# Moving one tile's industry product, stacking two-part operands on rows, and reordering the last tile of a layer in a four-layer graph kernel

## The chip, the cores and the metric

The kernel runs on one core of a Trainium2 chip. The metric is the device time of one execution in microseconds. A core has five engines that run side by side, each through its own instructions in order: TensorE (PE, with its weight loads shown apart as PEld), VectorE (DVE), ScalarE (ACT), GpSimd (POOL) and SyncE (SP), which here issues the DMA transfers. An engine waits at an instruction until the semaphores that it names are reached, and whatever stands behind that instruction on the same engine waits too.

## The reference, cut to what matters

There are B = 8 samples of N = 2048 nodes with C = 64 channels, and one sparse adjacency of 2048 x 2048, normalised by rows. Four layers follow each other, each as `x = layernorm(x + layer(x))`.

```python
# layer 0: Chebyshev terms T0=I, T1=A, T2=2AA-I, weights made per node from an embedding
w = einsum('nd,dkio->nkio', embedding, weight); x_g = einsum('knm,bmc->bnkc', A_stack, x)
out = einsum('bnki,nkio->bno', x_g, w) + bias
# layer 1: attention over 64 hyperedges (H: 2048 x 64), then "industry" against "g"
h = x @ W;  s = leaky_relu(h @ a_node)
alpha = softmax(where(H.T, s, NEG)); agg = einsum('ben,bnf->bef', alpha, h)   # per hyperedge
beta = sigmoid((h @ a_gn)[node] + (agg @ a_ge)[edge])
all_he = elu(beta * h + (1 - beta) * agg)                                     # per edge and node
he = elu(agg); se = tanh(he @ fcW + fcb) @ av; coefs1 = softmax(where(H, se, NEG))
g = einsum('bne,benf->bnf', coefs1, all_he)
industry = einsum('nm,bmf->bnf', adj / deg, x @ W_ind)
pair = stack([industry, g]); out = softmax(tanh(pair @ fcW + fcb) @ av) weighted sum of pair
# layer 2: x @ Ws + (adj @ x) @ Wn + b;   layer 3: (Dinv (adj + I) Dinv @ x) @ W.T
```

## The kernel before, in words

**Tiles.** A tile is 128 nodes (P), so there are NT = 16 of them; a tile's row of 8 samples times 64 channels is BC = 512 columns. Each large product takes its one operand as a 0/1 mask of the adjacency (a tile of it, 128 columns against all nodes, is 1 MB in a DRAM scratch, loaded by `mask_tile`, L1337) and the other as a pair "hi" and "lo" whose sum is the float32 value: each part is exact in TensorE's single-pass float32 format (`r_`, F32R), so two passes give full precision. A tile's industry product is therefore 32 matmuls of 128x128 by 128x512 (16 row blocks times two parts, `times_mask`).

**Stages in order.**

1. `first_product` and `memberships` (L306 on). The masks and layer 0's first product are made. Meanwhile, by quarters of 512 nodes, lists are built and stored in DRAM scratch: for each node its first to fourth hyperedge as one-hot columns (`oh01`: first and second, 64 rows each; `oh23`: third and fourth), a one-hot `S` for memberships beyond, and the transposed membership `pT`.
2. `layer0` (L923). A loop over j = 0..16 with steps g = 0..7 works on tile j (weights and sums, `weigh`) and finishes tile j-1 (`normed`, `to_features`, `scores`) and tile j-2 (`project`, `gather`). `scores` gives es, the exponentials of s; `project` (L1144) gives `h` and the pair y_hi, y_lo of x @ W_ind; `gather` (L1182) adds a tile to `aggp`, the numerator of agg; `denominators` (L1197) adds the 16 tiles' es to `denp`. In the last round, j = 16, denp's first 15 tiles stand at g = 1, behind `spread`, which makes the membership operands.
3. Stage 1 of `layer1` (L535 to L600): one chain over the 64 hyperedges, with each step on another engine. agg (DVE), he (ACT exponential, DVE), `trhe` (PE), heT (ACT), `fche` (PE), the (ACT tanh), `sep` (PE, 16 matmuls of one column), ese (DVE, ACT), its pair ese2 (DVE), `dnp` (PE, 16 matmuls), rec (ACT, DVE) and `hgr` (DVE reciprocal, L598). Beside it, `halves` splits agg + 1 and -agg into pairs, and `ext` collects two columns per sample for each hyperedge.
4. The turns of `layer1`. A string of steps (`turns`, L878) is run for t = 0..18; in turn t, tile t+1's unit (hyperedges to g), tile t's industry product, and the mixing and norm of tiles t-1 to t-3 go side by side. Tile 0's unit and the head of tile 1's go ahead of turn 0. A unit begins with `sx` (L633 to L637: the one-hots against ext, S against hgr) and goes on with `gp` in two halves (L680: a one-hot of 64 rows against the pair of agg, for two of the four lists side by side on rows 0 to 63 and 64 to 127), three DVE operations `d` each, `dp` (L705: float32 part; L707: the fourth list against the pair of -agg), exponentials, and sums on POOL. The industry's result is read by DVE's `dlt` (L750), which frees its accumulator for the next tile.
5. The tail of layer 1 makes layer 2's operands tile by tile (`tr`, `u`, L850, and the pair y_hi, y_lo, L858 and L860). Layers 2 and 3 (L1340 on) are 16 tiles each of 32 mask matmuls, and a norm.

**What sets the order.** `program_order` (L196) pins the order of PE, DVE, ACT and POOL to the order in which the program is written, inside layer 0's loop, stage 1 and the turns. SyncE's order is left to the scheduler. A transfer into on-chip memory waits until everything that used that memory is finished; pools opened one after another share memory, and buffers of one tag alternate in it. The PSUM accumulators are allotted in the same way.

A branch on `flag` chooses this program where no node has too many memberships; `bad` and `badp` (L1393) are part of that check.

Of the kernel before, what the change touches and what calls it, by code (L numbers as in the profile page):

```python
# [18 lines left out]
P = 128  # L19
# [32 lines left out]
def kernel(  # L52
# [176 lines left out]
    def lists_flag(box, tot, pm, w, an, avc):  # L229
# [56 lines left out]
        for k, shape in (  # L286
            ("oh01", [P, QW]), ("oh23", [P, QW]), ("S", [P, 4, P]), ("pT", [E, QW])
        )
# [6 lines left out]
    def memberships(pre, ps, pm, fcw_sb, fcb_sb, fcg_sb):  # L295
# [26 lines left out]
        raws = {}  # L322

# [22 lines left out]
        for q in range(NQ):  # L346

            raw = raws.pop(q)
            pT = pre.tile([P, QW], F32, tag="pT", name=f"pT_{q}")
            nc.vector.tensor_scalar(r_(pT), raw, 0.0, None, op0=ALU.is_gt)  # L350
            nc.sync.dma_start(lists["pT"][q], pT[0:E])
            yield
            pf = ps.tile([P, QW], F32, tag="li", name=f"pf_{q}")
            nc.tensor.matmul(
                pf, r_(tri.rearrange("p h e -> p (h e)")), r_(pT[0:E]), start=True, stop=True
            )
            yield
            pfm = raw
            nc.vector.tensor_tensor(pfm, pf, pT, ALU.mult)
            oh01 = pre.tile([P, QW], F32, tag="oh01", name=f"oh01_{q}")  # L360
            nc.vector.tensor_scalar(r_(oh01), pfm, order01, None, op0=ALU.is_equal)
            nc.sync.dma_start(lists["oh01"][q], oh01)
            oh23 = pre.tile([P, QW], F32, tag="oh23", name=f"oh23_{q}")
            nc.vector.tensor_scalar(r_(oh23[0:64]), pfm[0:64], 3.0, None, op0=ALU.is_equal)
            if q + 1 < NQ:
                load(q + 1)
            S = pre.tile([P, 4, P], F32, tag="S", name=f"S_{q}")
            yield
            for t in range(4):

                j = 4 * q + t
                cols = slice(t * P, (t + 1) * P)
                sm = ps.tile([P, QW], F32, tag="li", name=f"sm_{j}")
                nc.tensor.matmul(
                    sm[:, 0:E], r_(pT[0:E, cols]), r_(tri[:, 0, :]), start=True, stop=True
                )
                nc.vector.tensor_scalar(
                    r_(S[:, t, :]), iota[:, 0, :], base3[:, j:j + 1], None, op0=ALU.is_ge
                )
                nc.vector.scalar_tensor_tensor(  # L380
                    r_(S[:, t, :]), iota[:, 0, :], end3[:, j:j + 1], S[:, t, :],
                    op0=ALU.is_lt, op1=ALU.mult,
                )
                yield
                rk = pre.tile([P, 2, E], F32, tag="rk", name=f"rk_{j}")
                for h in range(2):
                    nc.vector.scalar_tensor_tensor(
                        r_(rk[:, h, :]), sm[:, 0:E], base3[:, j:j + 1], pm[:, j, :],
                        op0=ALU.add, op1=ALU.mult,
                    )  # L390
                yield
                nc.tensor.matmul(
                    sm[:, P:2 * P], r_(rk.rearrange("p h e -> p (h e)")), r_(S[:, t, :]),
                    start=True, stop=True,
                )
                yield
                nc.vector.tensor_tensor(
                    r_(oh23[64:128, cols]), sm[64:128, P:2 * P], iota[64:128, 1, :], ALU.is_equal
                )
            nc.sync.dma_start(lists["oh23"][q], oh23)  # L400
            nc.sync.dma_start(lists["S"][q], S)
            yield
# [92 lines left out]
    def layer1(  # L495
        stack, own, wts, fcw_sb, fcb_sb, av_sb, fcg_sb, vecs, rden, hgr, aggp, agg_st, h_sb,
        i_hi, i_lo, mask_tile, times_mask, w2_sb, bias2_sb,
# [8 lines left out]

        oh01 = l1.tile([P, N], F32, tag="oh01", name="oh01")
        oh23 = l1.tile([P, N], F32, tag="oh23", name="oh23")

        S = l1.tile([P, NT, P], F32, tag="S", name="S")  # L510

        agg_hi, agg_lo = (
# [6 lines left out]
        ext = l1.tile([P, 2, 2, B], F32, tag="ext", name="ext")  # L519

        with tc.tile_pool(name="fa", bufs=2) as fa:
            pT = fa.tile([E, N], F32, tag="pT", name="pT", bufs=1)
            for q in range(NQ):
                cols = slice(q * QW, (q + 1) * QW)
                nc.sync.dma_start(pT[:, cols], lists["pT"][q])
                nc.sync.dma_start(oh01[:, cols], lists["oh01"][q])
                nc.sync.dma_start(S[:, 4 * q:4 * q + 4, :], lists["S"][q])
                nc.sync.dma_start(oh23[:, cols], lists["oh23"][q])
# [5 lines left out]
            with program_order():  # L534
# [5 lines left out]
                nagg_hi, nagg_lo = (  # L540
                    own.tile([P, BC], F32, tag=f"b0_{k}", name=f"nagg_{k}") for k in (11, 15)
                )

                def halves(hi, lo, f, c):
                    s = slice(0 if c else 64, P)
                    nc.vector.tensor_scalar(r_(hi[s]), agg[s], f, c, op0=ALU.mult, op1=ALU.add)
                    full = fa.tile([P, BC], F32, tag="full", name="full", bufs=1)
                    nc.vector.tensor_scalar(full[s], agg[s], f, c, op0=ALU.mult, op1=ALU.add)
                    nc.vector.tensor_tensor(r_(lo[s]), full[s], hi[s], ALU.subtract)

                nc.vector.tensor_scalar(he, he, 1.0, -1.0, op0=ALU.min, op1=ALU.add)
                nc.vector.tensor_tensor(he, he, agg, ALU.max)
                tr = ps_tr.tile([P, NP, P], F32, tag="tr", name="trhe")
# [4 lines left out]
                halves(agg_hi, agg_lo, 1.0, 1.0)  # L558
# [10 lines left out]
                nc.gpsimd.memset(ext, 0.0)  # L569
# [9 lines left out]
                halves(nagg_hi, nagg_lo, -1.0, 0.0)  # L579
                ese2 = fa.tile([P, 2, B], F32, tag="ese2", name="ese2", bufs=1)  # L580
                nc.vector.tensor_copy(r_(ese2[:, 0, :]), ese)
                nc.vector.tensor_tensor(r_(ese2[:, 1, :]), ese, ese2[:, 0, :], ALU.subtract)

                dn = ps_tr.tile([P, NT, 2, B], F32, tag="tr", name="dnp")
# [5 lines left out]
                for h in range(2):  # L590
                    s = slice(h * 64, (h + 1) * 64)
                    nc.vector.tensor_reduce(ext[s, h, 0, :], b_view(he)[s], AX.X, ALU.add)
                    nc.vector.tensor_copy(ext[s, h, 1, :], ese[s])
# [29 lines left out]
        ps_acc = stack.enter_context(tc.tile_pool(name="fi", bufs=1, space=PSUM))  # L623
        ps_fc = stack.enter_context(tc.tile_pool(name="ff", bufs=1, space=PSUM))
        extv = ext.rearrange("p u k b -> p (u k b)")

        def units(j, dst):

            cols = slice(j * P, (j + 1) * P)
            sm = ps_s.tile([P, QW], F32, tag="sm", name=f"sx_{j}")  # L630

            for i in range(2):
                nc.tensor.matmul(  # L633
                    sm[:, P + 32 * i:P + 32 * i + 32], (oh01, oh23)[i][:, cols], extv,
# [40 lines left out]
            for i in range(2):  # L675
                gp = ps_g.tile([P, 2, BC], F32, tag="g", name=f"gp_{j}_{i}")
                for u in range(2):
                    rs = slice(u * 64, (u + 1) * 64)
                    for part in (agg_hi, agg_lo):
                        nc.tensor.matmul(  # L680
                            gp[:, u, :], r_((oh01, oh23)[i][rs, cols]), r_(part[rs]),
                            start=part is agg_hi, stop=part is agg_lo,
                        )
# [18 lines left out]
                if i == 0:  # L702
# [3 lines left out]
                    for part in (nagg_hi, nagg_lo):  # L706
                        nc.tensor.matmul(  # L707
                            dp, r_(oh23[64:128, cols]), r_(part[64:128]),
                            start=False, stop=part is nagg_lo,
                        )  # L710
# [25 lines left out]
        def industry(j):  # L736

            a = mask_tile(mjp, j, "l1")
            acc = ps_acc.tile([P, BC], F32, tag="acc", name=f"ind_{j}")
            for mt in range(NT):  # L740
                times_mask(acc, a, i_hi, i_lo, mt)
# [181 lines left out]
    def layer0(  # L923
# [6 lines left out]
        h_sb, wb, wa, vecs, av_sb, pm, es, hgr, aggp, rden = layer1s  # L930
# [157 lines left out]
        def normed(j, step):  # L1088
# [10 lines left out]
            elif step == 1:  # L1099
                var = tile("var", f"var_l0_{j}", (P, B))  # L1100
                nc.vector.tensor_reduce(var, b_view(norm[j]), AX.X, ALU.add)
                std = tile("std", f"std_l0_{j}", (P, B))
                nc.scalar.activation(std, var, AF.Sqrt, bias=eps_t)
                norm[j] = std
            else:
                rstd = tile("rstd", f"rstd_l0_{j}", (P, B))
                nc.vector.reciprocal(rstd, norm[j])
# [36 lines left out]
        def project(j):  # L1144
# [23 lines left out]
            nc.scalar.copy(r_(by_half(hi)), mm[:, :, :, C:2 * C])  # L1168
            nc.scalar.copy(by_half(h_sb[:, j, :]), mm[:, :, :, 0:C])
# [30 lines left out]

        denp = []
# [17 lines left out]
        with program_order():  # L1219
# [6 lines left out]
            for j in range(NT + 1):  # L1226
# [4 lines left out]
                for g in range(8):  # L1231
                    when(j, weigh, g)
                    if g == 0:
                        when(j - 1, normed, 0)
# [4 lines left out]
                    elif g == 1:  # L1239
                        when(j - 1, normed, 1)  # L1240
                        if j == NT:
                            denp.append(ps_acc.tile([P, BC], F32, tag="acc", name="denp")[:, 0:B])
                            spread()
                            denominators(0, NT - 1)
                        if first:
# [23 lines left out]
                    elif g == 6:  # L1269
# [4 lines left out]
                        else:  # L1274
                            denominators(NT - 1, NT)
# [5 lines left out]
            project(NT - 1)  # L1281
# [3 lines left out]
    def short_program(top):  # L1285
# [69 lines left out]
        agg_st = ExitStack()  # L1355
        with tc.tile_pool(name="l0", bufs=1) as l0, tc.tile_pool(
# [10 lines left out]
            h_sb = buffer(own, 1, "h")  # L1367
            aggp = agg_st.enter_context(tc.tile_pool(name="fag", bufs=1, space=PSUM)).tile(
                [P, BC], F32, tag="agg", name="aggp"
            )  # L1370
            with tc.tile_pool(name="l0s", bufs=2) as l0s, tc.tile_pool(
                name="accs0", bufs=1, space=PSUM
            ) as ps_acc, tc.tile_pool(name="trs0", bufs=2, space=PSUM) as ps_tr, tc.tile_pool(
# [4 lines left out]
                    y_hi, y_lo, (h_sb, wb, wa, vecs, av_sb, pm, es, hgr, aggp, rden),  # L1378
# [22 lines left out]
            y_lo, mask_tile, times_mask, w2_sb, bias2_sb,  # L1401
        )

# [671 lines left out]
```

## Time and profile before

| | us |
|---|---|
| three runs | 1355.73, 1354.02, 1349.54 |
| their median | 1354.02 |
| the profiled execution's own time | 1355.84 |
| its span in the trace | 1354.0 |
| PE busy in the span | 1287.4 (95%) |
| DVE busy | 917.9 (68%) |
| ACT busy | 367.0 (27%) |
| POOL busy | 443.7 (33%) |

The profiled execution has a span (first to last instruction) and a time of its own that is 1.8 us longer. Stages on the span's scale: layer 0 until about 699, its last tile until 720, stage 1 until 739, the turns until about 1047, the tail of layer 1 until 1086, layers 2 and 3 until the end. Each engine's busy time is given as a share of the span; the clock of TensorE as it was granted is a row of its own, in tenths of full speed; over the whole span it is 0.962. A name such as `gp<-agg,oh` reads "writes gp from agg and oh"; L680 is a line of the program. In a group, `x4` is four instructions; "idle before" names who released the engine.

### The profile page before, as it was taken

The page shows a single profiled execution, that of the slowest core. Times are in us where ns is not written, and L with a number is a line of the kernel's source. Part 1 is how long each engine was busy: PE and PEld are TensorE (multiplying, and loading weights), DVE is VectorE, ACT ScalarE, POOL GpSimd, SP SyncE. Part 2 cuts the span into 40 slices and gives each one's busy share as a digit, 9 for nine tenths or more (in the row PEclk, how much of TensorE's full clock was granted, in tenths as well). Part 3 has the DMA queues.
Part 4 walks back from the last instruction along what each step waited for, and adds up shares of the span by engine and source line. Part 5 has one row for each costly group of instructions (what it writes and reads, how often), then busy time and mean ns, then how long its engine had stood idle before and what let it go on. Part 6 is the DMA issues. An engine that isn't in the chain of part 4 may idle for free.

```text
span 1354.0 us, 19969 instructions
## 1 busy us (share of the span) xinstructions
PE 1287.4 (95%) x7788; PEld 1006.0 (74%) x7788; DVE 917.9 (68%) x1591; ACT 367.0 (27%) x840; POOL 443.7 (33%) x372
## 2 busy tenths in 40 slices
PE   6999999999999999999986799999998899999996
PEld 4777788888888888888874466666666678888885
DVE  3555378787877777777663677888884656655454
ACT  2100102112112222222221346666655611111111
POOL 2000354444444444444210455555663510000000
PEclk8999999999999999999985699999998899999999
DMA  9866432333333333331604121112220223334452
GB/s 217 264 193 193 150 112 89 104 104 104 104 105 104 104 104 104 104 104 55 233 25 155 55 78 68 66 62 78 78 79 1 94 93 125 124 119 140 169 186 73
DMA packets 91221, 153.02 MB, mean 113 GB/s; under 512 B 12272, under 2 KB 55664, under 8 KB 84848
## 3 DMA queue, kind: packets, MB, share of 16 engines
q1 hardware_dynamic: 88640, 147.45, 33.4%
q10 hardware_dynamic: 2304, 4.20, 0.8%
q8 instruction: 64, 1.05, 0.3%
q14 instruction: 37, 0.30, 0.1%
q0 software_dynamic: 176, 0.02, 0.1%
HBM read 115.98 MB, written 35.66 MB: 112 GB/s over the span
## 4 chain that ended last, share of the span: by engine, by line
PE 88%; DVE 5%; DMA 3%; ACT 2%; issue 1%; POOL 0%; SPq 0%; ACTq 0%; DVEq 0%; POOLq 0%
PE pp L1073 24%; PE a L1345 17%; PE ind L1345 10%; PE y2p L1036 9%; PE y1p L471 6%; PE fc L785 3%; PE df L794 2%; DMA xraw<-in_xn 2%; PE gp L680 2%; PE aggp L1182 1%; PE try L154 1%; PE trm L154 1%; PE yp L1433 1%; PE sgp L1130 1%; PE red L730 1%
## 5 line engine op out<-in xcount | busy, mean ns | idle before, releaser
L1084 DVE SCALAR_TENSOR_TENSOR r<-pp,emb_sb,r 128x256 f32<-128x256 f32 x512 | 247.3, 483 | 115.0 <-PE pp L1073 101.3
L1073 PE MATMUL pp<-w_sb,xT 64*128 64x256 f32 x1024 | 160.6, 390 | 1.7 <-DVE r L1084 1.7
L1073 PE MATMUL pp<-w_sb,y1T 64*128 64x256 f32 x1024 | 153.7, 376 | 0.0
L1073 PE MATMUL pp<-w_sb,y2T 64*128 64x256 f32 x1024 | 153.7, 376 | 0.0
L1022 POOL TENSOR_TENSOR r<-xs,bn 128x256 f32<-128x256 f32 x32 | 22.7, 731 | 385.7 <-issue 245.0
L471 PE MATMUL y1p<-x_hi,m 128*128 128x512 f32 x256 | 106.3, 415 | 14.1 <-ACT x_hi L418 13.3
L1073 PEld LDWEIGHTS pp<-w_sb,xT 64*128 64x128 f32 x1024 | 94.6, 187 | 25.0 <-issue 14.9
L721 POOL TENSOR_TENSOR ez<-ez,coef 128x1024 f32<-128x1024 f32 x32 | 65.0, 2032 | 139.2 <-DVE ez L719 116.8
L1073 PEld LDWEIGHTS pp<-w_sb,y1T 64*128 64x128 f32 x1024 | 99.9, 187 | 10.7
L1073 PEld LDWEIGHTS pp<-w_sb,y2T 64*128 64x128 f32 x1024 | 99.8, 187 | 10.8
L1345 PE MATMUL ind<-y_hi,mj_l 128*128 128x512 f32 x256 | 106.6, 416 | 0.4 <-DVE dlt L750 0.3
L1036 PE MATMUL y2p<-y_hi,msk 128*128 128x512 f32 x256 | 103.0, 402 | 0.0
L471 PE MATMUL y1p<-x_lo,m 128*128 128x512 f32 x256 | 103.0, 402 | 0.0
L1345 PE MATMUL a<-y_hi,mj_l 128*128 128x512 f32 x256 | 101.3, 396 | 0.6 <-ACT y_hi L858 0.6
L1345 PE MATMUL a<-y_lo,mj_l 128*128 128x512 f32 x256 | 101.3, 396 | 0.0
L1036 PE MATMUL y2p<-y_lo,msk 128*128 128x512 f32 x256 | 101.3, 396 | 0.0
L1345 PE MATMUL ind<-y_lo,mj_l 128*128 128x512 f32 x256 | 101.2, 395 | 0.0
L1345 PE MATMUL a<-v_hi,mj_l 128*128 128x512 f32 x256 | 100.2, 392 | 0.0
L1345 PE MATMUL a<-v_lo,mj_l 128*128 128x512 f32 x256 | 100.1, 392 | 0.0
L978 POOL TENSOR_TENSOR ms<-msk,srow 128x1024 f32<-128x1024 f32 x32 | 89.9, 2809 | 4.4 <-DVE ms L991 4.4
L1345 PEld LDWEIGHTS ind<-y_hi,mj_l 128*128 128x128 f32 x256 | 48.6, 190 | 32.8 <-issue 18.8
L471 PEld LDWEIGHTS y1p<-x_hi,m 128*128 128x128 f32 x256 | 49.5, 194 | 26.9 <-ACT x_hi L418 13.8
(265 smaller groups left out, 2393.7 us busy)
## 6 DMA issues: line engine op xcount, KB each, us to landing
mj_l<-mask SPq DMA_DIRECT2D x48, 1024.0 KB, 4.9
raw<-in_at SPq DMA_DIRECT2D x32, 512.0 KB, 4.7
adj<-in_at SPq DMA_DIRECT2D x64, 256.0 KB, 3.8
mask<-msk SPq DMA_DIRECT2D x32, 512.0 KB, 4.4
xraw<-in_xn SPq DMA_DIRECT2D x8, 512.0 KB, 5.3
oh<-oh SPq DMA_DIRECT2D x16, 256.0 KB, 3.7
xT<-in_xt SPq DMA_DIRECT2D x16, 256.0 KB, 3.0
xs<-in_xn SPq DMA_DIRECT2D x16, 256.0 KB, 2.9
```

Of the source, the lines that this page charges most:

```text
L154: nc.tensor.matmul(dst, src, ident, start=True, stop=True, is_transpose=True)
L471: nc.tensor.matmul(accs[q][jj], r_(m[:, t, jj * P:(jj + 1) * P]), r_(part[:, mt, :]), start=i + h + t == 0 and part is x_hi, stop=i == 3 a ...
L680: nc.tensor.matmul(gp[:, u, :], r_((oh01, oh23)[i][rs, cols]), r_(part[rs]), start=part is agg_hi, stop=part is agg_lo,)
L721: nc.gpsimd.tensor_tensor(by_b(ez), by_b(ez), per_b(coef, 2 * i, 2), ALU.mult)
L785: nc.tensor.matmul(fc[:, h, :], fcw_sb[rs], sT[rs], start=True, stop=True)
L794: nc.tensor.matmul(df[:, b:b + 1], th[:, b % 2, (b // 2) * P:(b // 2 + 1) * P], av_sb, start=True, stop=True,)
L978: nc.gpsimd.tensor_tensor(ms, m, srow[j].unsqueeze(1).to_broadcast([P, 8, P]), ALU.mult)
L1022: nc.gpsimd.tensor_tensor(r[:, 4 * bq * C:4 * (bq + 1) * C] .rearrange("p (h l c) -> p h l c", h=2, l=2), swapped(terms[j]["xs"], bq), bn. ...
L1036: nc.tensor.matmul(acc, r_(msk[j, mt // 8][:, mt % 8, :]), r_(part[:, mt, :]), start=mt == 0 and part is y_hi, stop=mt == NT - 1 and part ...
L1073: nc.tensor.matmul(pp[:, h, pl, :], terms[j][name][rs, 2 * bq + pl], w_sb[rs, k, dq * 4 * C:(dq + 1) * 4 * C], start=k == 0, stop=k == K - 1,)
L1084: nc.vector.scalar_tensor_tensor(rb, ppv[:, :, dd, :], emb_sb[:, j, d:d + 1], rb, op0=ALU.mult, op1=ALU.add)
L1345: nc.tensor.matmul(acc, r_(a[:, mt, :]), r_(part[:, mt, :]), start=mt == 0 and part is hi, stop=mt == NT - 1 and part is lo,)
```

## The change: what it does

1. **Lists.** `oh01` and `oh23` of a quarter become one list `oh` of 128 rows by 4 tiles by 4 one-hots by 128 nodes. Each one-hot of 64 rows is stored twice, in rows 0 to 63 and in rows 64 to 127, by `store`. The eight loads of the whole lists before stage 1 go; each unit loads its own tile, 256 KB, into one of four buffers of the pool `fw`.
2. **Stacked parts.** agg + 1, -agg and ext are kept as one tile each, with the rounded value in rows 0 to 63 and the residual in rows 64 to 127. A `gp` half becomes two matmuls of 128 rows for four of 64, `dp`'s second part one for two, and `sx`'s products with ext four in the single-pass format for two in float32.
3. **Industry's tile 0.** Its 32 matmuls leave turn 0. Its mask is loaded in four pieces into buffers of layer 0, and `go_on(n)` issues n pairs: 5 behind denp's first part, 3 ahead of the last gather, 4 ahead of trhe, 1 ahead of fche, 2 ahead of sep, 1 ahead of dnp. Its accumulator's pool lives from layer 0 through the turns, and denp takes a slot of layer 0's projection pool.
4. **Layer 0's last tile.** `spread` stands one step earlier (g = 0); project(15) stands right behind scores(15), and copies `h` ahead of y_hi; the norm's 1/sqrt is DVE's addition of EPS and GpSimd's power, where the other tiles use ScalarE's root and DVE's reciprocal.
5. **Small ones.** The split of -agg stands behind dnp's issue; ext is formed in a tile `sums` and split by `parts`; GpSimd's memset of ext goes.

```diff
+        def store(q, oh, first):
+            for h in range(2):
+                for u in range(2):
+                    nc.sync.dma_start(
+                        lists["oh"][q][h * 64:(h + 1) * 64, :, first + u, :],
+                        oh[u * 64:(u + 1) * 64].rearrange("e (t n) -> e t n", t=4),
+                    )
...
-            nc.sync.dma_start(lists["oh01"][q], oh01)
+            store(q, oh01, 0)
...
-            nc.sync.dma_start(lists["oh23"][q], oh23)
+            store(q, oh23, 2)
...
-                def halves(hi, lo, f, c):
-                    s = slice(0 if c else 64, P)
-                    nc.vector.tensor_scalar(r_(hi[s]), agg[s], f, c, op0=ALU.mult, op1=ALU.add)
+                def parts(dst, full):
+                    nc.vector.tensor_copy(r_(dst), full)
+                    nc.vector.tensor_tensor(r_(dst[low]), full[low], dst[low], ALU.subtract)
+                def scaled_parts(dst, f, c):
                     full = fa.tile([P, BC], F32, tag="full", name="full", bufs=1)
-                    nc.vector.tensor_scalar(full[s], agg[s], f, c, op0=ALU.mult, op1=ALU.add)
-                    nc.vector.tensor_tensor(r_(lo[s]), full[s], hi[s], ALU.subtract)
+                    nc.vector.tensor_scalar(full, agg, f, c, op0=ALU.mult, op1=ALU.add)
+                    parts(dst, full)
...
+                early[0](4)
                 tr = ps_tr.tile([P, NP, P], F32, tag="tr", name="trhe")
...
-                halves(agg_hi, agg_lo, 1.0, 1.0)
+                scaled_parts(agg1, 1.0, 1.0)
+                early[0](1)
                 fc = ps_mm.tile([P, 2, QW], F32, tag="mm", name="fche")
...
-                nc.gpsimd.memset(ext, 0.0)
+                early[0](2)
                 sp = ps_tr.tile([P, QW], F32, tag="sm", name="sep")
...
-                halves(nagg_hi, nagg_lo, -1.0, 0.0)
                 ese2 = fa.tile([P, 2, B], F32, tag="ese2", name="ese2", bufs=1)
...
+                sums = fa.tile([P, 2, B], F32, tag="sums", name="sums", bufs=1)
+                nc.vector.tensor_reduce(sums[:, 0, :], b_view(he), AX.X, ALU.add)
+                nc.vector.tensor_copy(sums[:, 1, :], ese)
+                parts(ext, sums)
+                early[0](NT)
                 dn = ps_tr.tile([P, NT, 2, B], F32, tag="tr", name="dnp")
...
+                scaled_parts(nagg, -1.0, 0.0)
...
         def units(j, dst):
-            cols = slice(j * P, (j + 1) * P)
+            oh = small("oh", f"oh_{j}", (P, 4, P), 4)
+            nc.sync.dma_start(oh, lists["oh"][j // 4][:, j % 4])
...
-            for i in range(2):
+            for u in range(4):
                 nc.tensor.matmul(
-                    sm[:, P + 32 * i:P + 32 * i + 32], (oh01, oh23)[i][:, cols], extv,
+                    sm[:, P + 16 * u:P + 16 * u + 16], r_(oh[:, u, :]), r_(extv),
...
-                    rs = slice(u * 64, (u + 1) * 64)
-                    for part in (agg_hi, agg_lo):
-                        nc.tensor.matmul(
-                            gp[:, u, :], r_((oh01, oh23)[i][rs, cols]), r_(part[rs]),
-                            start=part is agg_hi, stop=part is agg_lo,
-                        )
+                    nc.tensor.matmul(
+                        gp[:, u, :], r_(oh[:, 2 * i + u, :]), r_(agg1), start=True, stop=True
+                    )
...
-                    for part in (nagg_hi, nagg_lo):
-                        nc.tensor.matmul(
-                            dp, r_(oh23[64:128, cols]), r_(part[64:128]),
-                            start=False, stop=part is nagg_lo,
-                        )
+                    nc.tensor.matmul(dp, r_(oh[:, 3, :]), r_(nagg), start=False, stop=True)
...
         def industry(j):
-            a = mask_tile(mjp, j, "l1")
-            acc = ps_acc.tile([P, BC], F32, tag="acc", name=f"ind_{j}")
+            if j:
+                a = mask_tile(mjp, j, "l1")
+                acc = ps_acc.tile([P, BC], F32, tag="acc", name=f"ind_{j}")
+            else:
+                acc = early[1]
             for mt in range(NT):
-                times_mask(acc, a, i_hi, i_lo, mt)
+                if j:
+                    times_mask(acc, a, i_hi, i_lo, mt)
...
+                if j == NT - 1:
+                    nc.vector.tensor_scalar(var, var, EPS, None, op0=ALU.add)
+                    rstd = tile("rstd", f"rstd_l0_{j}", (P, B))
+                    nc.gpsimd.tensor_tensor(rstd, var, mhalf, ALU.pow)
+                    norm[j] = rstd
+                    return
...
+            for q, home in enumerate((4, 6, 13, 14)):
+                m = own.tile([P, 4, P], F32, tag=f"b0_{home}", name=f"m0_{q}")
+                nc.sync.dma_start(m, masks[0][:, 4 * q:4 * q + 4, :])
...
                         if j == NT:
-                            denp.append(ps_acc.tile([P, BC], F32, tag="acc", name="denp")[:, 0:B])
-                            spread()
+                            denp.append(
+                                ps_p.tile([P, 2, 2, 4 * C], F32, tag="pp", name="denp")[:, 0, 0, 0:B]
+                            )
                             denominators(0, NT - 1)
+                            early.extend(industry_early())
+                            early.pop(0)(5)
...
                         else:
+                            project(NT - 1, h_first=True)
                             denominators(NT - 1, NT)
                             gather(NT - 2)
...
-            project(NT - 1)
+            early[0](3)
             gather(NT - 1)
```

## Prediction

> **What bounds the kernel now.** I read the slices of the span first, then the chain of waits from 699 to 772 us, the windows of equal length around it, TensorE's timeline in one steady turn, and SyncE's issues. Times are microseconds of the span.
>
> ```profile
> PE   6999999999999999999986799999998899999996
> PEclk8999999999999999999985699999998899999999
> PE 88%; DVE 5%; DMA 3%; ACT 2%; issue 1%; POOL 0%; SPq 0%; ACTq 0%; DVEq 0%; POOLq 0%
> ```
>
> The second line is the granted TensorE clock in tenths. PE is nearly always busy; the one hole is at slices 21 to 23 (710 to 765 us), where busy share and clock both fall. That is the chain from the end of layer 0 to the first turns of layer 1, and most of the change lands there.
>
> ```profile
> 702.76 0.63 ACT sq_l L1097
> ...
> 709.76 1.28 ACT L1142
> ...
> 713.86 3.13 issue
> 717.02 1.05 POOL hs L1177
> 718.12 2.09 PE aggp L1182 x2
> 720.21 2.71 issue
> ...
> 738.36 0.96 DVE hgr L598
> 739.37 0.61 PE sx L637 x2
> ...
> 755.62 1.23 PE gp L680 x4
> ...
> 761.39 3.71 PE ind L1345 x8
> ```
>
> Columns: start, duration, what. L1142 is a table load; the 3.13 us of "issue" is project(15) behind the gather of tile 14. Eight industry matmuls cost 3.71 us, 0.46 each; where the clock is full they start 0.228 apart.
>
> ```profile
> 700.36:703.77 3.41, 3.29 (x36) 3.08 (x35) 2.53 (x5) 0.99 (x2) 0.00 (x0) 1.00 0.19 68
> 703.77:707.18 3.41, 1.11 (x4) 0.67 (x4) 1.96 (x5) 2.40 (x5) 1.04 (x1) 0.50 0.10 35
> ...
> 761.80:765.21 3.41, 3.41 (x10) 2.18 (x11) 1.23 (x1) 2.60 (x11) 1.35 (x1) 0.50 0.00 0
> 765.21:768.62 3.41, 3.41 (x15) 2.22 (x16) 2.60 (x3) 0.00 (x0) 1.84 (x2) 1.00 0.00 0
> ```
>
> Columns: window, length, busy time of PE, PEld, DVE, ACT, POOL, clock, DMA share, GB/s. The clock changes on a grid of 3.41 us. It halved at 703.77 after a window that PE filled for 3.29 us, but mostly with `denp`'s matmuls of 8 columns (699.04 to 702.49); it came back at 765.21 after a window filled with 512-column industry matmuls. So what counts is columns streamed: I work with "falls after a window under about half filled by wide matmuls, returns after one filled throughout".
>
> ```profile
> 843.94 0.73 PE L680 MATMUL gp<-agg,oh 64*128 64x512 f32 x4
> ...
> 848.44 0.73 PE L707 MATMUL dp<-nagg,oh 64*128 64x512 f32 x2
> 849.18 0.50 PE L1345 MATMUL ind<-y_hi,mj_l 128*128 128x512 f32 x1
> ```
>
> A steady turn takes 17.42 us (gp at 843.94, next at 861.36) and PE is full. But the industry group at 849.18 also needs DVE's dlt, which ended at 849.12 (848.38 + 0.74): both routes from gp to the industry tie within 0.06 us.
>
> **The change, part by part** (sum against the profiled run, 1355.84 us for a span of 1354.0; it stands 1.8 above the median 1354.02).
>
> *A, layer 0's tail until aggp's end (720.19).* Ten industry matmuls stand after denp, hp_15 right behind the scores, six between the two gathers; POOL's power (row L823: 1.67) and an addition replace table load 1.28 + root 0.30 + reciprocal 0.20; the table load before es goes. At full clock: denp ends 702.49, ten industry 2.3, hp_14 1.16; x1 is ready at var's end 704.1 + 0.17 + 1.67 + two halves 0.8 = 706.7; trx 0.58, xT 0.6, sgp 0.95, hp_15 1.16, denp 0.3, aggp 1.03, six industry 1.4, aggp 1.03: about 713.75, so -6.4. At half clock from 703.77: the ten industry end at 705.6, hp_14 2.08, trx 1.11, xT 0.7, sgp 1.87, hp_15 2.08, denp 0.60, aggp 2.0, industry 2.56, aggp 2.07: 720.7, so +0.5. denp fills its window with narrow matmuls as before, so I take the fall and **0** (-6.4 to +1.8, the upper end if all ten run slow).
>
> *B, aggp's end to hgr (19.1 us before).* The dense stretch denp to aggp (714 to 720.7) brings the clock back about where stage 1 begins. Then trhe gains 0.55, fche 1.04, sep 1.8, and ese2 no longer stands behind nagg's three operations on DVE (731.90 to 733.38): 1.5. agg starts 0.8 later, because DVE gets the badp and flag operations ahead of it, whose PE part now follows aggp. dnp follows sep's narrow matmuls, so I leave it slow. Sum **-4.1**; all slow it is 0 (the -1.5 eaten by 0.8 and by industry groups of 0.86 to 1.7 that outlast the waits of 0.73 and 1.27 they fill), all at full clock -6.
>
> *C, oh_0's load.* The list was resident; now each unit loads 256 KB. The compiled order of waits shows that oh_0's issue waits for hgr, the last operation of stage 1, since the buffer takes memory that stage 1 holds.
>
> ```profile
> 739.44 0.79 SPq L1340 DMA_DIRECT2D mj_l<-mask  x2
> ...
> 1070.43 1.27 SPq L1340 DMA_DIRECT2D mj_l<-mask  x3
> ```
>
> SyncE's timeline above, the page's row of DMA issues below (KB each, median us to landing):
>
> ```profile
> oh<-oh SPq DMA_DIRECT2D x16, 256.0 KB, 3.7
> ```
>
> Before, the mask issue had that wait (739.44, just behind hgr's 739.31) and nobody needed it until 761. sx_0 needs oh_0 at once: issue 0.1, landing 3.0 to 3.7 (rows of 256 KB), then sx on ext (1.06 at half clock), which before lay ahead of hgr. **+4.3** (3.0 to 4.9). Later units load a turn or more ahead and cost nothing.
>
> *D, turns 0 and 1.* Without industry, turn 0 (16.77 us) is its unit's own chain: about -1.4, since gp of the next unit stood 0.8 behind its DVE release and gp1 of this one stood behind the eight slow industry matmuls. But those matmuls brought the clock back. Now turn 1 starts slow: its rows from 772.32 to 777.81, 5.5 us, take 9.2, and part of eight industry matmuls 0.20 more each: +5. **+3.6** (-1.4 if the clock is up anyway, to +5.5).
>
> *E, fourteen further turns.* gp: four matmuls occupy 0.67, two full ones 0.34 + 0.23 = 0.57 by the industry's rows (one switch, one follow-up). dp's second part: 0.74 to about 0.3. sx on ext: 0.36 to 0.44 (four narrow ones at 0.11, as df). PE's route to the industry shrinks by 0.47, but DVE's (gp, three d of 1.23, dlt) only by gp's 0.1, and it ties; gp1 gives another 0.1 behind it. Per turn 0.2 to 0.3: **-3.6** (-1.5, up to -14 if all 0.95 counted). Three turns (809, 898, 987) took 19.0 because the clock dropped for one window; a turn near 17.15, almost five windows, drifts less against that grid: **-3** (-4.7 to +5).
>
> The Trainium skill, "TensorEngine Tiling (Array Packing)", Tiling Modes, speaks against the stacking: tiles of 64 rows execute in parallel, so two half-height pairs cost what two full matmuls do. The row of 0.67 for four (not 4 x 0.228) agrees; by the page alone gp would gain nothing, by the row 0.1.
>
> *F, the first mask of layer 2.* By the order of waits its issue now waits for u_15, the last matmul of layer 1 (ends 1085.27), in place of POOL's rstd_15; it went out at 1070.43, and layer 2 started at 1085.88. A megabyte takes 4.9 (median of 48), the least I found 4.8: +4.3, with nothing else for PE. A gap of 4.9 always leaves a window under half filled; the clock falls and the next filled window ends 3.7 to 7.1 us after the restart, which costs half of it: 1.85 to 3.55. **+7.0** (4.3 to 8.2).
>
> The Trainium skill, "TensorE: Matmul & The Clock Gate", Part 1, has half rate after an idle window of 3413 ns on a free-running grid. The grid agrees; the window up to 703.77 was not idle, and there the measurement decides. By the page this gap holds a whole idle window in (4.9 - 3.41)/3.41, 4 of 10 phases, and F would be about 5.4.
>
> *G, the lists' stores.* 24 more issues at 0.33 us on SP at 60 to 110 us, with runs of 512 B; the raw loads run two ahead: **+1** (0 to 3).
>
> Sum: 0 - 4.1 + 4.3 + 3.6 - 3.6 - 3 + 7 + 1 = +5.2, so 1361.0.
>
> **Rivals.**
> 1. *The turns are bound by PE alone* (other side: no longer slower). Then each turn gives 0.95, -13.3 in place of -3.6: 1351. For it: PE is 256 of 258 us busy from 772 to 1030, DVE 206. Against: the tie at 849.12, and turn 1's industry waited 0.26 for dlt. It decides from 0.65 per turn.
> 2. *The fill keeps the clock up* through A and B: -12.4 in place of -4.1: 1352.7. For it: 26 dense matmuls in the gaps. Against: denp's 3.45 us of narrow matmuls ahead of them, sep's behind. Both together: 1343.
> 3. *The fill does not do what it says*: matmuls at 0.43 delay trx and trhe, A +1.8, B 0, G +3: 1369.
>
> **How the numbers follow.** Forecast 0.50 (own range 1354 to 1367), rival 1 0.14, rival 2 0.16, both 0.05, rival 3 0.15. 0.5%, about 6.8 us, is what a measurement of this kernel can tell: faster is below 1347.2, slower above 1360.8. Faster: both rivals, a third of each alone, a little of the forecast's tail: 0.19. Slower: somewhat over half of the forecast, rival 3: 0.43. Same: 0.38. Range 1346 to 1369: low takes in rivals 1 and 2, high rival 3.
>
> **What would show it.** After: hgr about 735, then a SyncE issue behind it and gp_0 over 4 us later (C); the clock at half until turn 1's industry (D); SyncE's first layer-2 mask issued at u_15's end, PE idle near 5 us, and eight or more slow matmuls behind it (F); steady turns of 17.1 to 17.2 with DVE's dlt as releaser of the industry (E); fewer than three half-clock windows in 772 to 1030. Wrong if gp_0 starts before 737, if layer 2 starts within 1 us of u_15, or if turns fall below 16.8.

## The result, and the profile after

The changed kernel took 1351.13 us (median of 12 runs, 1346.22 to 1358.69), the kernel before 1354.08 (12 runs, 1349.54 to 1359.3). The ratio is 0.9984, with a 95% interval of 0.9967 to 1.0002: no difference that this measurement can tell, where 1361 was forecast. The profiled execution after took 1354.48, its span is 1352.5.

The page of the kernel after, the same three rows (busy share of PE, granted clock, chain):

```profile
PE   6999899999999999999997599999998799999997
PEclk8999899999999999999986599999998899999999
PE 85%; DVE 8%; DMA 3%; ACT 2%; issue 1%; SPq 0%; POOL 0%; ACTq 0%; DVEq 0%; POOLq 0%
```

The hole around slice 22 is there as before, and DVE's share of the whole chain has grown from 5% to 8%. The chain of waits through the hole (start, duration, what):

```profile
700.06 4.15 PE denp L1212 x30
704.21 4.47 PE ind L1229 x10
...
728.08 1.95 PE sep L576 x16
...
731.08 3.52 PE dnp L594 x16
...
735.50 0.96 DVE hgr L603
...
737.90 3.73 DMA oh<-oh
...
771.41 1.19 PE gp L685 x2
...
774.84 2.01 PE fc L789 x4
...
778.95 1.86 PE ind L1395 x8
```

The ten early industry matmuls ran at half clock (4.47 us, 0.45 each), sep ran at full clock (1.95; 3.58 before), dnp at half, and behind hgr stands a DMA that was not in the chain before. In turn 1, from 771.41, fc is slow and the industry is fast: 1.86 for eight.

Set side by side on each span's own scale, with the shift that had built up by each landmark (the letters are the terms of the forecast):

| landmark | before | after | shift | step |
|---|---|---|---|---|
| denp starts | 699.04 | 699.99 | +0.95 | |
| aggp ends | 720.19 | 720.69 | +0.50 | A -0.45 |
| hgr ends | 739.31 | 736.45 | -2.86 | B -3.4 |
| gp of unit 0 | 740.20 | 741.11 | +0.91 | C +3.8 |
| gp, turn 0 | 755.62 | 755.38 | -0.24 | unit 0 -1.15 |
| gp, turn 1 | 772.32 | 771.41 | -0.91 | turn 0 -0.7 |
| gp, turn 2 | 790.02 | 790.43 | +0.41 | turn 1 +1.3 |
| gp, turn 14 | 1003.93 | 996.32 | -7.61 | twelve turns -8.0 |
| last u of layer 1 ends | 1085.25 | 1077.23 | -8.02 | |
| layer 2 starts | 1085.87 | 1082.24 | -3.63 | mask +4.4 |
| end | 1354.02 | 1352.48 | -1.54 | restart +2.1 |

So a gain of 8 us in the later turns and 3.9 in the chain is for the most part given back at two places, where a transfer is waited for. SyncE's and PE's timelines of the second one:

```profile
1077.38 15.56 SPq L1390 DMA_DIRECT2D mj_l<-mask  x4
```

```profile
1076.07 1.16 PE L854 MATMUL u<-w_sb,xT 64*128 64x128 f32 x16 [0.42 <-DVE y_lo L864]
1082.24 0.76 PE L1395 MATMUL a<-y_hi,mj_l 128*128 128x512 f32 x1 [5.01 <-DMA mj_l<-mask]
1082.80 0.63 PE L1395 MATMUL a<-y_lo,mj_l 128*128 128x512 f32 x1
...
1088.33 0.40 PE L1395 MATMUL a<-y_hi,mj_l 128*128 128x512 f32 x1
```

The last u ends at 1077.23, the mask is issued at 1077.38, and the first matmul that needs it starts 4.86 later; then fourteen matmuls run at half clock until 1088.3.

### The profile page after: what moved, and what is told of

Its sections match the earlier page's. It is cut to its first block, busy times and chain, and to the rows that moved or that the text cites. A ratio compares the mean times of both kernels' runs of the same rounds, so it can differ in the third digit from the quotient of the medians.

```text
span 1352.5 us, 19863 instructions
## 1 busy us (share of the span) xinstructions
PE 1273.8 (94%) x7708; PEld 1009.9 (75%) x7708; DVE 917.2 (68%) x1592; ACT 363.9 (27%) x837; POOL 445.2 (33%) x372
## 4 chain that ended last, share of the span: by engine, by line
PE 85%; DVE 8%; DMA 3%; ACT 2%; issue 1%; SPq 0%; POOL 0%; ACTq 0%; DVEq 0%; POOLq 0%
PE pp L1077 24%; PE a L1395 18%; PE y2p L1040 9%; PE ind L1395 9%; PE y1p L478 8%; PE df L798 2%; PE fc L789 2%; DMA xraw<-in_xn 2%; DVE d L698 1%; DVE d L702 1%; DVE d L694 1%; PE gp L685 1%; PE try L154 1%; PE yp L1485 1%; PE hp L1165 1%
## 5 line engine op out<-in xcount | busy, mean ns | idle before, releaser
L1077 PEld LDWEIGHTS pp<-w_sb,xT 64*128 64x128 f32 x1024 | 94.4, 186 | 25.1 <-issue 14.9
L1395 PE MATMUL ind<-y_hi,mj_l 128*128 128x512 f32 x240 | 97.5, 406 | 6.9 <-DVE dlt L754 6.9
L1395 PE MATMUL ind<-y_lo,mj_l 128*128 128x512 f32 x240 | 94.5, 394 | 0.0
L1395 PEld LDWEIGHTS ind<-y_hi,mj_l 128*128 128x128 f32 x240 | 45.4, 189 | 35.5 <-DVE dlt L754 14.4
```

The lines of the kernel that those rows point to most:

```text
L1077: nc.tensor.matmul(pp[:, h, pl, :], terms[j][name][rs, 2 * bq + pl], w_sb[rs, k, dq * 4 * C:(dq + 1) * 4 * C], start=k == 0, stop=k == K - 1,)
L1395: nc.tensor.matmul(acc, r_(a[:, mt, :]), r_(part[:, mt, :]), start=mt == 0 and part is hi, stop=mt == NT - 1 and part is lo,)
```

## The experiments

All ratios are against the kernel before on the same chip, five rounds each. Between two variants I compare ratios, with 0.001 = 1.35 us; each has an interval of some +-0.002 to 0.003.

**e1: unit 0's one-hots in a buffer of their own.**

```diff
+        oh0 = l1.tile([P, 4, P], F32, tag="oh0", name="oh0")
...
+            nc.sync.dma_start(oh0, lists["oh"][0][:, 0])
...
-            oh = small("oh", f"oh_{j}", (P, 4, P), 4)
-            nc.sync.dma_start(oh, lists["oh"][j // 4][:, j % 4])
+            if j:
+                oh = small("oh", f"oh_{j}", (P, 4, P), 4)
+                nc.sync.dma_start(oh, lists["oh"][j // 4][:, j % 4])
+            else:
+                oh = oh0
```

> The changed kernel, with the first unit's one-hots loaded into a buffer of their own ahead of stage 1, so that nothing waits for hgr. Theory (the load is a wait of its own): gp_0 starts 1.0 us behind hgr's end in place of 4.65 (741.11 - 736.46), the clock is still at half there, and the time falls by about 3.7 against the changed kernel. Rival (the wait covers another): sx waits for ext, S or ScalarE in its place and gp_0 moves by under 1 us; or gp_0 moves by 3.7 but turn 1 starts slower, and under 1 us of it reaches the first turn at full clock.

Measured: 1343.52, ratio 0.9925 (0.9898 to 0.9953), 8 us under the changed kernel. PE's timeline:

```profile
731.08 1.02 PE L645 MATMUL sx<-ext,oh 128*128 128x16 f32 x4
733.23 0.60 PE L649 MATMUL sx<-hgr,S 128*128 128x16 f32 x2 [1.13 <-DVE hgr L605]
...
733.78 1.20 PE L690 MATMUL gp<-agg,oh 128*128 128x512 f32 x2
```

sx on ext is ahead of hgr again, and gp starts 0.61 behind hgr's end (733.17) in place of 4.66: -4.05, so the load was a wait of its own. Stage 1 was shorter as well, 13.62 in place of 15.76. DVE's timelines, after and then e1, tell 0.8 of that:

```profile
720.84 0.16 DVE L1445 TENSOR_SCALAR bad<-badp 128x1 f32<-128x1 f32 x1 [3.82 <-PE badp L1444]
...
721.50 0.69 DVE L537 TENSOR_TENSOR agg<-aggp,rden 128x512 f32<-128x512 f32 x1
```

```profile
719.59 0.69 DVE L539 TENSOR_TENSOR agg<-aggp,rden 128x512 f32<-128x512 f32 x1 [2.45 <-PE aggp L1202]
720.20 0.15 DVE L1450 TENSOR_SCALAR bad<-badp 128x1 f32<-128x1 f32 x1
```

The flag's operations, whose place the scheduler chooses, stand behind agg here and ahead of it after. Another 1.25 is dnp, which ran mostly at full clock (2.18 in place of 3.58; DVE's split of -agg, until 731.61, then ends last in its place). One profile can't tell if that is more than the place of the clock's windows. The profiled run took 1348.41, 4.9 above the median of the eight, and its span is 6.1 under that of the profile after. So of the 8 us by the runs the trace shows 4.05 for the load and 2.1 for stage 1; what the rest is, it can't show.

**e2: the first mask of layer 2.**

```diff
-        with tc.tile_pool(name="mj2", bufs=3) as mjp, tc.tile_pool(
+        with tc.tile_pool(name="mj2a", bufs=1) as mja, tc.tile_pool(
+            name="mj2b", bufs=1
+        ) as mjb, tc.tile_pool(name="mj2c", bufs=1) as mjc, tc.tile_pool(
...
-                a = mask_tile(mjp, j, "l2")
+                a = mask_tile((mja, mjb, mjc)[j % 3], j, "l2")
...
-                a = mask_tile(mjp, j, "l3")
+                a = mask_tile((mja, mjb, mjc)[(NT + j) % 3], j, "l3")
```

> The changed kernel, with three single-buffer pools for the masks of layers 2 and 3, so that the first one overlaps only memory that is free once the last unit is done. Theory: the first mask is issued 14 us or more ahead of u_15's end, layer 2 starts within 1 us of u_15 at full clock, idle time of 4.4 and some 2 us of slow matmuls behind it go: -6.5 against the changed kernel. Rival (only the idle goes, the clock falls there anyway, since it had been at half until 1071): -4.4. Second rival: the earlier transfer collides with the tail's, which then ends later, and nothing is gained.

Measured: 1344.6, ratio 0.992 (0.9889 to 0.9951), 8.7 under the changed kernel. SyncE, then PE:

```profile
1061.70 14.41 SPq L1390 DMA_DIRECT2D mj_l<-mask  x3
```

```profile
1074.10 1.16 PE L854 MATMUL u<-w_sb,xT 64*128 64x128 f32 x16 [0.42 <-DVE y_lo L864]
1075.88 0.47 PE L1395 MATMUL a<-y_hi,mj_l 128*128 128x512 f32 x1 [0.63 <-ACT y_hi L862]
```

The wait is gone, and the first matmul runs at full clock. From the last u's end to the end of the span it is 268.4 us, against 275.25 after: -6.8, which is the price that the forecast gave step F (7.0). The other 2.0 us between the two spans lie ahead of the last u. Both rivals fall.

**e3: both.** The edits of e1 and e2 together.

```diff
+            nc.sync.dma_start(oh0, lists["oh"][0][:, 0])
...
+                a = mask_tile((mja, mjb, mjc)[j % 3], j, "l2")
```

> Both edits, the one-hots of unit 0 and the three mask pools. Theory: they lie 340 us apart and add up, -10 against the changed kernel, 1341 or so, faster than both kernels. Rival (either is taken back by a later wait): between -4 and -7.

Measured: 1337.54, ratio 0.9874 (0.9844 to 0.9905): faster than both kernels, 14.9 under the changed one. Within the intervals the two add up (8.0 + 8.7), and neither is taken back.

**e7: gp in halves again.**

```diff
-                    nc.tensor.matmul(
-                        gp[:, u, :], r_(oh[:, 2 * i + u, :]), r_(agg1), start=True, stop=True
-                    )
+                    rs = slice(u * 64, (u + 1) * 64)
+                    for part in (agg1, agg2):
+                        nc.tensor.matmul(
+                            gp[:, u, :], r_(oh[rs, 2 * i + u, :]), r_(part[rs]),
+                            start=part is agg1, stop=part is agg2,
+                        )
```

> The changed kernel with gp alone as before (four matmuls of 64 rows for two of 128, from a pair agg1, agg2); dp and sx stay stacked. Theory (a switch between half-height and full-height matmuls costs about 0.1 on each side, and only gp1 counts, because the DVE chain ties at gp0): the steady turn goes from 16.96 back to 17.3 to 17.4. Rival (dp's second part gives the turn's gain): it stays near 17.0 to 17.1. By the forecast's own rows (0.1 for gp1): 17.05.

Measured: 1356.3, ratio 1.0026 (1.0000 to 1.0051), 5.7 over the changed kernel, with intervals that just touch; the steady turn takes 17.46, as before the change (17.42), against 16.96. The whole gain of the turn is gp's, and none is dp's or sx's. PE's timelines around gp1, in e7 and then after:

```profile
852.89 0.39 PE L1401 MATMUL ind<-y_lo,mj_l 128*128 128x512 f32 x1
853.21 0.74 PE L690 MATMUL gp<-agg,oh 64*128 64x512 f32 x4
853.87 0.50 PE L1401 MATMUL ind<-y_hi,mj_l 128*128 128x512 f32 x1
854.21 0.40 PE L1401 MATMUL ind<-y_lo,mj_l 128*128 128x512 f32 x1
```

```profile
846.59 0.50 PE L1395 MATMUL ind<-y_hi,mj_l 128*128 128x512 f32 x1 [0.57 <-DVE dlt L754]
...
848.31 0.40 PE L1395 MATMUL ind<-y_lo,mj_l 128*128 128x512 f32 x1
848.54 0.62 PE L685 MATMUL gp<-agg,oh 128*128 128x512 f32 x2
849.00 0.40 PE L1395 MATMUL ind<-y_hi,mj_l 128*128 128x512 f32 x1
849.24 0.39 PE L1395 MATMUL ind<-y_lo,mj_l 128*128 128x512 f32 x1
```

From the last industry matmul ahead of gp to the second one behind it are 1.32 us in e7 (0.32 + 0.66 + 0.34) and 0.93 after (0.23 + 0.46 + 0.24). Half-height matmuls cost about 0.1 at each change of shape, into them and out of them, beside 0.2 of their own. The first line after shows the tie that the forecast saw: the industry waits 0.57 for DVE's dlt, so dp's saving and most of gp0's are lost there.

**e4: no early industry.** industry(0) as before, in turn 0; everything else as changed.

```diff
-                            early.extend(industry_early())
-                            early.pop(0)(5)
...
-            if j:
-                a = mask_tile(mjp, j, "l1")
-                acc = ps_acc.tile([P, BC], F32, tag="acc", name=f"ind_{j}")
-            else:
-                acc = early[1]
+            a = mask_tile(mjp, j, "l1")
+            acc = ps_acc.tile([P, BC], F32, tag="acc", name=f"ind_{j}")
```

> The changed kernel with industry's tile 0 back in turn 0, as one mask of 1 MB; stacking and the tail's order stay. Theory (the fill removes PE work from turn 0, whose unit is bound by its own chain, and keeps the clock up only in parts of stage 1): aggp ends 2 to 3 us earlier than in the changed kernel, hgr 0 to 2 us later, turn 0 takes 16.5 to 17 in place of 16.0, turn 1 about 17.3 in place of 19.0; the sum is within 2 us of the changed kernel. Rival (the fill is what brings stage 1's clock back, worth 4 or more): aggp to hgr takes 18 to 19 in place of 15.8 and the time rises by 3 or more.

Measured: 1349.03, ratio 0.9961 (0.9936 to 0.9987). aggp ends 19.85 behind denp's start (20.70 after), stage 1 takes 17.84 (15.76), turns 0 and 1 take 15.22 and 17.35 (16.03 and 19.02). In the windows (length, busy PE, PEld, DVE, ACT, POOL, clock, DMA share, GB/s) of turns 0 and 1, with the turn in which the clock came back in two parts, e4 first, then after:

```profile
755.05:760.80 5.75, 5.75 (x16) 4.18 (x17) 5.48 (x6) 0.48 (x3) 3.15 (x2) 0.51 0.00 0
760.80:770.27 9.47, 8.24 (x34) 6.12 (x33) 6.22 (x10) 4.50 (x14) 4.11 (x3) 1.00 0.08 28
770.27:787.62 17.35, 16.30 (x82) 11.44 (x80) 12.11 (x15) 8.41 (x19) 10.57 (x7) 1.00 0.30 100
```

```profile
755.38:771.41 16.03, 7.61 (x16) 4.04 (x17) 12.09 (x16) 5.55 (x17) 6.37 (x5) 0.50 0.05 16
771.41:777.69 6.28, 6.28 (x21) 4.25 (x22) 5.14 (x5) 1.43 (x2) 5.28 (x3) 0.50 0.15 44
777.69:790.43 12.74, 12.74 (x61) 9.28 (x60) 7.58 (x11) 6.40 (x17) 5.50 (x4) 1.00 0.12 30
```

With the industry in turn 0 the clock is back at 760.7; without it PE is slow for all of turn 0 and 6.3 us of turn 1, and turn 0 is no shorter. What the fill gains in stage 1 (2.1) it loses in these two turns (2.5). The rival's stage 1 came (17.84), its loss of time did not.

**e5: lists and stacking alone.** e4's edit, and besides the root by ScalarE, `spread` at g = 1 and project(15) at the end, as before.

```diff
-                            project(NT - 1, h_first=True)
                             denominators(NT - 1, NT)
...
+            project(NT - 1)
             gather(NT - 1)
```

> Lists, stacked parts and the small edits alone: no early industry, spread, project(15) and the ScalarE root as in the kernel before. Theory: against the kernel before, the turns give 0.4 to 0.47 each (some -6), the load of the one-hots behind hgr +3.8 and the late mask +4 to +6.5: +2 to +4 in all. Against the variant without the fill it shows the tail's order alone: its aggp ends 3 to 4 us later. Rival (the tail's order gives nothing, because half clock stretches whatever follows): aggp ends within 1 us of that variant.

Measured: 1353.42, ratio 0.9988 (0.9962 to 1.0015), -1.6 in place of +2 to +4. It has both new waits (4.67 from hgr to gp, 5.05 ahead of layer 2), and the shorter turns. It also shows a gain that I had not counted, in PE's rows of gp:

```profile
742.61 1.20 PE L681 MATMUL gp<-agg,oh 128*128 128x512 f32 x2
756.88 1.19 PE L681 MATMUL gp<-agg,oh 128*128 128x512 f32 x2 [4.01 <-DVE ez L715]
772.11 0.63 PE L681 MATMUL gp<-agg,oh 128*128 128x512 f32 x2
```

Unit 0, turn 0 and turn 1 take 14.27, 15.23 and 17.32, against 15.42, 16.70 and 17.70 before, 3.0 in all. In turn 0, at half clock, PE reaches the first industry matmul 4.52 us into the turn (5.70 before), and the second gp then waits for DVE's ez, at 8.31 (9.41 before). Against e4, aggp ends 0.4 later behind denp's start, so the rival holds in the profile; by the runs e4 is 3.7 better, with overlapping intervals, and that stays unclear.

**e8: ScalarE's root.** The last tile's norm as in the other tiles.

```diff
-                if j == NT - 1:
-                    nc.vector.tensor_scalar(var, var, EPS, None, op0=ALU.add)
-                    rstd = tile("rstd", f"rstd_l0_{j}", (P, B))
-                    nc.gpsimd.tensor_tensor(rstd, var, mhalf, ALU.pow)
-                    norm[j] = rstd
-                    return
```

> The changed kernel with the last tile's root by ScalarE and its reciprocal by DVE, as in the other tiles; all else stays. Theory (x1 is ready before PE asks for it either way, and es is not asked for until hp_15 ends): the end of aggp moves by under 0.7 us, the time by less than can be seen. Rival (the table load ahead of es is on the path): aggp ends 1.3 us later.

Measured: 1349.74, ratio 0.9963 (0.9939 to 0.9987); aggp ends 20.93 behind denp's start, against 20.70: +0.2. The root's engine does not matter by these profiles, as the theory has it; the runs' intervals overlap.

**e9: both waits mended, no early industry.** e3's and e4's edits.

```diff
+            nc.sync.dma_start(oh0, lists["oh"][0][:, 0])
...
+                a = mask_tile((mja, mjb, mjc)[j % 3], j, "l2")
...
-                            early.extend(industry_early())
-                            early.pop(0)(5)
```

> Both waits mended (one-hots of unit 0 in a buffer of their own, three mask pools), and industry's tile 0 back in turn 0. Theory (the fill shortens the chain to hgr by 1 to 4, and loses 2.5 or more in turns 0 and 1, where the industry brought the clock back one turn earlier): within 2 us of the variant with both waits mended and the fill, 1335.5 to 1339.5. Rival (the fill pays once the wait behind it is gone, since its clock now reaches the units): 4 us slower, 1341 or more.

Measured: 1340.79, ratio 0.9906 (0.9889 to 0.9922), 4.3 over e3, next to the rival's 1341. Its stage 1 takes 17.84 against 13.62, its turns 0 and 1 32.55 against 35.65. With the waits in place leaving out the fill gained 3.1 (e4), without them it loses 4.3; in each pair the intervals overlap. What the whole fill is worth by itself, these two pairs do not settle.

**e10: both waits mended, ten pairs in the gaps, six in turn 0.** On top of e3:

```diff
-                            early.pop(0)(5)
+                            early.pop(0)
...
-                early[0](NT)
...
+                elif mt < 6:
+                    early[0](1)
```

> Both waits mended, ten of the sixteen pairs of industry's tile 0 in the gaps from the last gather on, none behind denp, six pairs in turn 0. Theory (twelve matmuls in turn 0 are enough to bring the clock back there, and the ten behind denp were slow, 4.5 us on the path): aggp ends 2 to 4 us earlier where the clock had fallen, turn 1 takes about 17.4 in place of 19.6: 3 to 5 us under the variant with all of the fill. Rival (the six pairs lengthen turn 0 by what turn 1 gains, and the chain loses its clock): no gain.

Measured: 1336.28, ratio 0.9871 (0.9854 to 0.9887): no different from e3. Turn 0 took 14.70 and ran its last part at full clock, but the clock fell again at 760.9 and turn 1 took 20.41. The expectation of 17.4 was wrong: twelve industry matmuls bring the clock back and do not hold it, for behind them PE waits for DVE's ez and is busy for 0.52 of the 3.41 us up to 760.9. Against e9, measured on the same chip, the time is 4.7 lower (0.9871 against 0.9906), and every run of e10 (1335.1 to 1338.2) lies below every run of e9 (1339.8 to 1342.5). So with both waits mended, moving ten pairs into the gaps pays.

## Why the prediction was wrong, step by step

A slowdown of 5 us was forecast. The medians differ by -3, and the interval (-4.5 to +0.3) takes in zero, so no slowdown came, and a gain isn't shown either. The two waits, on which the forecast rested, came as forecast. What failed is the other side of the sum, in two terms: D, which priced turn 1 too high and put the stacking's gain in the first, slow tiles at nothing, and E, which put gp1's saving at 0.1 a turn, where it is 0.40.

- **D, turns 0 and 1 (+3.6 forecast; -0.5 measured with unit 0).** In the forecast's own terms, turn 1's +5 came as +1.3, turn 0's -1.4 as -0.7, and unit 0, which was not in the sum, gave -1.15. Turn 1's rows ahead of the industry took 7.4 us and not 9.2, and its industry was not slow. The step "now turn 1 starts slow" is right for the early industry: after against e4 it costs 2.5 from unit 0 to turn 1, e3 against e9 3.1. What it left out is that the stacking shortens the very same stretch by 3.0 (e5 against before). I had counted the stacking only for "fourteen further turns". Also "those matmuls brought the clock back" was too narrow: after, it came back at 777.69, ahead of any industry, behind a window of fc and transposes.
- **E, the further turns (-3.6 forecast; -5.6 measured, twelve turns of 0.47).** The mis-sized term is gp1: "four matmuls occupy 0.67, two full ones 0.57" left the gaps on both sides out. With them it is 1.32 against 0.93, so 0.40 and not 0.1; e7, which puts gp alone back, takes the turn back to 17.46. The rows were there in the profile before: 850.90 to 851.22 and 851.89 to 852.23, 0.32 and 0.34 where 0.228 is usual. The Trainium skill, "TensorEngine Tiling (Array Packing)", Key Properties, has it that changing the tiling mode drains TensorE; e7's rows agree, with about 0.1 on each side. I drew on the same part of that page and weighed only its parallel tiles. The tie with DVE is right (0.57 at dlt). Time lost in the turns to windows of low clock: 4.7 us before and 2.4 after, near the forecast's -3.
- **A (0; -0.45)** is near the 0 that was taken. That aggp ended at 720.69, where the half-clock working had 720.7, is luck: denp started 0.95 later, and the clock was up from 709.4 to 712.8. Rival 2 (the fill keeps the clock up) came up for this stretch in e3's profile, where aggp ended 14.85 behind denp's start; there the clock didn't fall until 726.
- **B (-4.1; -3.4)**: the terms for trhe, fche, sep, ese2 and the 0.8 for agg all show. e1 shows that the 0.8 is the scheduler's choice and not a consequence of the order on PE.
- **C (+4.3; +3.8 in the profile, 4.05 removed by e1)** and **F (+7.0; 4.4 + 2.1 in the profile, 6.8 removed by e2)** are right in mechanism and size. I had counted the gap as always costing the clock: with it (after, e1) the clock fell at layer 2's start, without it (e2, e3) it did not.
- **G (+1)** can't be seen: denp's start lies between 697.8 and 700.6 in all the traces.

Rival 1 (the turns bound by PE alone) is refused by the 0.57 wait for dlt; that its 1351 is the measured median is luck. Its 0.95 a turn does not follow from the forecast's rows (0.47 and 0.1 make 0.57), though PE's own work did shrink by about 1.04 a turn: the 0.47 that were gained and the 0.57 that PE now waits. Of the signs that were named, "wrong if turns fall below 16.8" did not occur, but the turns (16.95) lie under the 17.1 to 17.2 that were named for them. At the other places the profile looks as forecast, save that the clock was back about 1 us ahead of turn 1's industry. D and E make up some 6 of the 6.7 us between the sum (+5.2) and the profile (-1.5).

## What to carry to other kernels

When a change moves a buffer from resident to loaded, or makes a pool smaller, list which memory each later pool now lies over: here both new waits (4.05 and 6.8 us in the profiles, 8 to 9 each by the runs) came from that, and a buffer or a pool of its own removed them. When a group of matmuls changes its shape, time it from the neighbour ahead to the neighbour behind, since the change of shape is paid outside of its own rows. And when an edit applies to every tile, price it in the first, slow tiles too, not only in the steady turn.

## What the runs showed of the hardware

- **A hundredth of a microsecond decided over 1.1.** In unit 0, DVE's second d operation (L694 before, L698 after) and POOL's `g` start at the same time. GpSimd's rows and DVE's, before:

```profile
749.87 1.26 POOL L725 TENSOR_TENSOR g<-ez 128x512 f32<-128x512 f32 x1
```

```profile
749.89 1.79 DVE L694 SCALAR_TENSOR_TENSOR d<-gate,d 128x512 f32<-128x512 f32 x1
```

  and after:

```profile
750.76 1.80 POOL L725 TENSOR_TENSOR g<-ez 128x512 f32<-128x512 f32 x1
```

```profile
750.75 0.69 DVE L698 SCALAR_TENSOR_TENSOR d<-gate,d 128x512 f32<-128x512 f32 x1
```

  Whoever starts second is longer, by 1.1 (DVE) or 0.5 (POOL). e7, with POOL ahead by 0.01 again, has 1.79 and a unit 0 of 15.42. The Trainium skill, "SBUF — State Buffer", section "two separate sides", calls the port pair that these two engines share an exclusive lock, held for a whole instruction by whoever starts first, when a DVE operation has two inputs in SBUF (the on-chip memory), as this one has, and GpSimd's reads SBUF. These rows agree: whoever is second ends 0.55 (DVE) or 1.12 (POOL) behind the end of the first. They are 1.15 of the 3.0 that the forecast missed.
- **The clock follows wide matmuls, not busy time.** The share of a 3.41-us window with matmuls of 128 columns or more was 0.34, 0.26, 0.40 and 0.43 ahead of four falls (before at 703.8; after at 702.6, 712.8 and 729.9), though PE was busy for 0.96, 1.00, 0.68 and 0.96 of them; a window at 0.41 in e3 (from 699.0) and one at 0.51 after (from 856.2) did not fall. In all eleven traces, from 690 to 1100 us, the clock fell 74 times, each time behind a window with a share of 0.57 or less, and no window under 0.41 kept it. It came back behind windows of 0.79 to 1.0, but not behind all of these: before, the window from 758.4 to 761.8 was full of wide matmuls, and the clock stayed at half. So the forecast's "returns after one filled throughout" is not the whole rule, and what is missing is open.
